# Adjacency graph layers on one Trainium2 core: three edits to the order of work between the second pass and the block layer

## The chip, the cores and the metric

The kernel runs on one core of a Trainium2 chip. The metric is device time in microseconds. The core has five engines that work side by side: TensorE (PE in the profile, its weight loads PEld), VectorE (DVE), ScalarE (ACT), GpSimd (POOL) and SyncE (SP), which here only issues DMAs. [...]

## The reference

Four graph layers over one 2708 x 2708 adjacency matrix `adj` and 2708 x 128 features `x`, each followed by a residual and a layer norm. The edits lie where the first layer ends and the second is prepared, so only these two are shown:

```python
# layer 0: neighbours by distance of z, then a Laplacian product
z = leaky_relu(lap_mul(A, x) @ W1 + b1, 0.1)
S = exp(-dist(z) / 2), kept for the 4 largest of each row
x = layernorm(x + lap_mul(S + A, x) @ W2 + b2)

# layer 1: attention of rank one, normalised by A
XW = X @ W
s_col, s_row = XW @ a[:128], XW @ a[128:]
den = exp(leaky_relu(s_row[:, None] + s_col[None, :], 0.01))
num = A @ den
att = where(num != 0, den / num, 0)
x = layernorm(X + A @ (att @ XW))
```

Layers 2 and 3 are a normalised product with `adj` and a linear map each.

## The kernel before, in words

**Tiles and chunks.** The 2708 nodes are 22 tiles `t` of 128 (the last has 20 nodes) and six chunks `c` of columns: four of 512, one of 384 and one of 276. Chunk index 3 (`C - 3`) holds tiles 12 to 15, index 4 (`C - 2`, the fifth chunk) tiles 16 to 18, and index 5, the last, tiles 19 to 21.

**First and second pass.** The first pass over `adj` finds z and the four neighbours. The second pass (`by_panels`, L189 to L229, with products at L204) multiplies `adj` with the scaled features, chunk by chunk. The work that ends a chunk is not done at once: `end_pass2` (L993) puts it into a list `due` with a number for each step, and one step of the list is taken after each product of the pass. Steps with one number run in the order in which they were put in. Inside this stretch the order on TensorE, VectorE and ScalarE is the order in which the program issues (`manual_schedule`, L1036).

**Ending a chunk.** For each chunk but the last: `finish` copies the accumulator, `norm0` (L797) adds the residual and normalises, `turn` (L814) transposes the rows with TensorE and copies them to `xT` with ScalarE (L821), `find_c` (L869) multiplies them with the column vector into the row of c (`c_row`, L872 and its copy L873) and takes each node's own c out of it (L877). Then for each tile `compare` (L899) writes a 0/1 mask over all columns so far (one compare, L904, and one for ties within the tile, L914), `times_w` (L882) makes the tile's rows of X W (L885 and their copy L886), `rank_rows` (L919) adds up the mask along its rows on ScalarE (L922, a copy with an accumulated sum), and `rank_columns` (L924) does so along columns on TensorE (L927). These sums are the ranks by which nodes are sorted. The masks have four buffers; the PSUM tiles of `mis_tile` have three.

**The last chunk** isn't normalised first. `last_stats` finds mean and variance, GpSimd the power for `rstd_l` (L253), and `last_rc` (L843) corrects two columns of products to c and then r (L847 and L850, twice each). `turn_c` (L861) turns c into a row, which ScalarE copies (L867); `negate_r` follows. Then come `compare`, `rank_rows` and `rank_columns` of tiles 19 and 20, `compare_few` for the last 20 nodes, and the ranks.

**Third pass.** `adj` is read a third time, in 32 half rows of 128 x 1354 through 11 buffers and ten more half rows that stay in SBUF (`res`). `line(n)` multiplies the next n loaded half rows with `lc` (L1387, four column groups) and, where a buffer is used again, issues its next load on SyncE's queue. `own_line(n)` does so with resident ones, without a load. Between them, in an order written out in the list `turns` (L1482), TensorE does what prepares the block layer: `last_xw` makes the last three tiles' rows of X W (transpose L1180, copy L1182, product L1184, copy L1186, a DMA on GpSimd's queue to DRAM), `in_rank_order` and `in_list_order` sort by products with 0/1 matrices (L1228), `counts`, `ranks_known`, `next_weights`.

**Block layer.** `block_layer` (L1639) runs 44 steps of products (L1654), reciprocals on ScalarE, a Newton step on VectorE and products (L1536). Then come three more panel passes for the rest of layers 1 to 3.

## Time and profile before

| | us |
|---|---|
| median of 3 runs | 1071.4 |
| lowest, highest | 1069.7, 1076.45 |
| the profiled execution | 1068.27 |
| its span, first to last instruction | 1066.5 |
| TensorE matmul busy | 983.9 (92%) |
| TensorE weight loads busy | 481.8 (45%) |
| VectorE busy | 637.6 (60%) |
| ScalarE busy | 331.9 (31%) |
| GpSimd busy | 264.9 (25%) |
| mean granted TensorE clock | 0.971 |

The stages that matter here, in us from the start of the span: the second pass's last chunks from about 380 to 437, the last chunk's c, masks and ranks from 437 to 454, the third pass from 454.3 to 506.8, the block layer from 507.5 to 728.8.

In the rows of a timeline, the first number is the start in us, the second the length; then engine, line, operation, the tile written and the tiles read, the shape, and how many instructions are merged. What stands in brackets is the engine's idle time before the row and what ended it. The granted clock is the share of full speed that TensorE is given; it is listed for any stretch one asks for.

### The profile page before, as it was taken

To read this page: it belongs to the slowest core of one execution; us is meant where nothing else is said; L and a number is where in the kernel's file an instruction comes from. 1 tells how busy PE (TensorE), PEld (TensorE's weight loads), DVE (VectorE), ACT (ScalarE), POOL (GpSimd) and SP (SyncE) were. 2 spreads that over 40 slices of the span, in tenths; PEclk is the share of its full clock that TensorE was granted. 3 is DMA by queue.
4 is the path that set the end of the run, shared out by engine and by line. 5 is a ranking of instruction groups with operands and counts; after the bars stand their busy time and mean duration, and the time that the engine had idled before them with its cause. 6 is when DMAs were issued, how large, how long until landed. Compare 5 with 4: busy or idle time off the path is not lost.

```text
span 1066.5 us, 11660 instructions
## 1 busy us (share of the span) xinstructions
PE 983.9 (92%) x3773; PEld 481.8 (45%) x3773; DVE 637.6 (60%) x1363; ACT 331.9 (31%) x609; POOL 264.9 (25%) x339
## 2 busy tenths in 40 slices
PE   0888999999994998799899999999999999999996
PEld 0346544444442556654333333334445544564444
DVE  5985438999943578674798999995121121222222
ACT  0000126555500244612776776663010100010000
POOL 4000000000564565005766443430121100000000
PEclk9989999999997999699999999999999999999998
DMA  9998350000183666587565455456755856484652
GB/s 338 363 340 268 114 160 1 0 1 1 42 278 113 202 184 209 199 357 260 144 172 150 137 141 165 133 169 202 232 189 173 292 181 216 145 276 145 229 166 74
DMA packets 102001, 191.00 MB, mean 179 GB/s; under 512 B 14022, under 2 KB 43342, under 8 KB 101930
## 3 DMA queue, kind: packets, MB, share of 16 engines
q1 hardware_dynamic: 83896, 152.34, 43.1%
q0 software_dynamic: 17728, 37.62, 12.8%
q8 instruction: 32, 0.52, 0.2%
q14 instruction: 39, 0.32, 0.1%
q10 hardware_dynamic: 306, 0.20, 0.1%
HBM read 214.80 MB, written 4.16 MB: 205 GB/s over the span
## 4 chain that ended last, share of the span: by engine, by line
PE 48%; DVE 1%; ACT 1%; issue 0%; DMA 0%; POOL 0%; SPq 0%; POOLq 0%
PE acc L204 27%; PE hacc L1536 10%; PE num L1654 9%; PE mis L285 1%; PE mis L1783 0%; DMA ring<-carry 0%; ACT gb L234 0%; PE mis L1749 0%; DVE inv L1525 0%; PE mis L1779 0%; DVE inv L1528 0%; ACT inv L1511 0%; POOL rstd L253 0%; DVE err L1521 0%; PE mis L1737 0%
## 5 line engine op out<-in xcount | busy, mean ns | idle before, releaser
L1095 POOL DMA_INDIRECT ring<-in_adjT,slot_i x88 | 96.6, 1098 | 93.8 <-PE num L1654 72.1
L1654 PE MATMUL num<-ring,lw 128*64 128x512 f32 (+1 forms) x528 | 111.9, 550 | 4.0 <-DVE err L1521 1.9
L1536 PE MATMUL hacc<-inv,xws 128*128 128x512 f32 (+1 forms) x264 | 111.7, 559 | 1.7 <-ACT xws L1699 1.4
L705 PE MATMUL acc<-zT,z 128*128 128x512 f32 (+2 forms) x252 | 102.2, 552 | 0.0
L1511 ACT ACTIVATE inv<-num,plain 128x1024 f32<-128x1024 f32 x88 | 80.5, 915 | 59.3 <-PE num L1654 38.9
L253 POOL TENSOR_TENSOR rstd<-rstd,minus_half 128x4 f32<-128x4 f32 (+1 forms) x18 | 17.3, 959 | 313.5 <-DVE rstd L252 313.5
L234 ACT COPY gb<-acc 128x512 f32<-128x512 f32 (+2 forms) x18 | 9.6, 534 | 251.1 <-PE acc L204 251.1
L706 ACT COPY key<-acc 128x512 f32<-128x512 f32 (+2 forms) x126 | 67.1, 534 | 55.1 <-PE acc L705 27.7
L204 PE MATMUL acc<-ring,y 128*128 128x512 f32 (+2 forms) x192 | 83.3, 564 | 0.5 <-issue 0.5
L750 POOL DMA_INDIRECT got<-y_rows,where x66 | 70.8, 1073 | 45.8 <-DVE near_sum L763 25.9
L1536 PEld LDWEIGHTS hacc<-inv,xws 128*128 128x128 f32 x264 | 46.5, 189 | 78.7 <-issue 53.4
L1521 DVE TENSOR_TENSOR err<-inv,num 128x1024 f32<-128x1024 f32 x88 | 73.8, 852 | 10.2 <-DMA carry<-m_rows 4.9
L204 PE MATMUL acc<-ring,xs 128*128 128x512 f32 (+2 forms) x192 | 77.6, 547 | 0.0
L1528 DVE SCALAR_TENSOR_TENSOR inv<-gb,g_inv,inv 128x1024 f32<-128x1024 f32 x88 | 77.0, 912 | 0.1
L204 PE MATMUL acc<-ring,carry 128*128 128x512 f32 (+2 forms) x192 | 74.5, 542 | 0.0
L204 PE MATMUL acc<-ring,m_rows 128*128 128x512 f32 (+2 forms) x192 | 74.3, 542 | 0.0
L1525 DVE SCALAR_TENSOR_TENSOR inv<-err,inv 128x1024 f32<-128x1024 f32 x88 | 72.2, 858 | 0.1
L705 PEld LDWEIGHTS acc<-zT,z 128*128 128x128 f32 x252 | 45.8, 190 | 50.4 <-issue 45.0
L1514 ACT ACTIVATE inv<-inv 128x1024 f32<-128x1024 f32 x88 | 67.6, 768 | 2.8
L575 POOL TENSOR_TENSOR slot_e<-near,sim 128x44 f32<-128x44 f32 (+2 forms) x3 | 0.7, 238 | 259.3 <-DVE near L572 259.2
L709 DVE MAX8 near<-key 128x8 f32<-128x2708 f32 x21 | 62.3, 2965 | 2.6 <-ACT key L706 2.6
L1654 PEld LDWEIGHTS num<-ring,lw 128*64 128x64 f32 x528 | 35.6, 136 | 62.4 <-issue 44.6
(378 smaller groups left out, 1368.9 us busy)
## 6 DMA issues: line engine op xcount, KB each, us to landing
ring<-in_adjT SPq DMA_DIRECT2D x74, 1024.0 KB
ring<-in_adjT SPq DMA_DIRECT2D x20, 677.0 KB
ring<-in_adjT SPq DMA_DIRECT2D x17, 768.0 KB
part<-in_adjT SPq DMA_DIRECT2D x12, 1024.0 KB
ring<-in_adjT SPq DMA_DIRECT2D x17, 552.0 KB
more<-in_adjT SPq DMA_DIRECT2D x10, 677.0 KB
res<-in_adjT SPq DMA_DIRECT2D x4, 1280.0 KB
part<-in_adjT SPq DMA_DIRECT2D x3, 768.0 KB
```

The costliest lines, as they stand in the source:

```text
L204: nc.tensor.matmul(accs[c][: lhsT.shape[-1], :w], lhsT=lhsT, rhs=src, start=start, stop=stop)
L705: nc.tensor.matmul(pks[c][:p, : cw[c]], lhsT=z2[:, :p], rhs=zT[:, cs], start=False, stop=True)
L706: nc.scalar.copy(key[:p, cs], pks[c][:p, : cw[c]])
L750: nc.gpsimd.indirect_dma_start(out=got[:p, :], out_offset=None, in_=y2_rows[:, :], in_offset=bass.IndirectOffsetOnAxis(ap=where[:p, t, k : ...
L1095: nc.gpsimd.indirect_dma_start(out=rows[i][:KC, n, :], out_offset=None, in_=adj_half[:, :], in_offset=bass.IndirectOffsetOnAxis(ap=slot_i[ ...
L1511: nc.scalar.activation(inv, num[:, :w], AF.Ln, scale=plain[:, 0:1], bias=plain[:, 1:2])
L1514: nc.scalar.activation(inv, inv, AF.Exp, scale=-1.0)
L1521: nc.vector.tensor_mul(err, inv, num[:, :w])
L1525: nc.vector.scalar_tensor_tensor(inv, err, 2.0, inv, op0=ALU.subtract, op1=ALU.mult)
L1528: nc.vector.scalar_tensor_tensor(inv, gb[:, col : col + w], g_inv[:, q : q + 1], inv, op0=ALU.max, op1=ALU.mult)
L1536: nc.tensor.matmul(haccs[:, o:e], lhsT=xws[:, q, :], rhs=inv[:, o:e], start=(q == 0), stop=(q == NQ - 1))
L1654: nc.tensor.matmul(num[n * (BJ + 2) : (n + 1) * (BJ + 2), o:e], lhsT=lw[:, 2 * q + n, :], rhs=rows[i][:, n, c0 + o : c0 + e], start=True, ...
```

## The change

Three edits to the order, all in the stretch that ends with the third pass.

**Tile 15's sum.** For chunk index `C - 3` the sum along rows of its last tile is no longer put in at its own number but kept in `behind_turn`, and put in for chunk `C - 2` at the number of `find_c`, behind it. (The kernel did so already with the sum of chunk `C - 2`'s last tile, through `behind_last`.)

**Tile 19's compare.** `last_rc` is cut into `last_of`, called once for c and once for r. After c and the start of `turn_c`, `compare_known` compares tile 19 with all columns ahead of the last chunk, whose c is known; `compare` does only the other 128 columns for this tile. r and its negative come behind that.

**X W of the last tiles.** `last_xw` is cut into `turn_last` (transpose and copy) and `last_xw` (product, copy and DMA) of one tile each. Between a tile's transpose and its product stands a half row: the seventh of the loaded ones for tile 19, an own one for each of tiles 20 and 21. The own ones come out of the group of four that followed later.

```diff
-    def last_rc():
-        both = rc_of(C - 1, lambda t: P)
-        for v, dst in ((1, cc), (0, rr)):
-            nc.vector.scalar_tensor_tensor(
-                dst[:, l0:l1], mv[:, l0:l1, 0], w_sum[:, v : v + 1], both[:, v, :], op0=ALU.mult, op1=ALU.subtract
-            )
...
+    unscaled = []
+
+    def last_of(v, dst):
+
+        if not unscaled:
+            unscaled.append(rc_of(C - 1, lambda t: P))
+        nc.vector.scalar_tensor_tensor(
+            dst[:, l0:l1], mv[:, l0:l1, 0], w_sum[:, v : v + 1], unscaled[0][:, v, :], op0=ALU.mult, op1=ALU.subtract
+        )
...
+    def compare_known(t):
+        masks[t] = sum_pool.tile([P, N], BF16, tag="mask", name="mask", bufs=4)
+        nc.vector.tensor_scalar(
+            masks[t][:, : l0 * P], c_row[:, : l0 * P], cc[:, t : t + 1], None, op0=ALU.is_ge
+        )
+
     def compare(t):
         p, o = pw[t], t * P
         s = cc[:p, t : t + 1]
-        mask = masks[t] = sum_pool.tile([P, N], BF16, tag="mask", name="mask", bufs=4)
+        e = l0 * P if t in masks else 0
+        if not e:
+            masks[t] = sum_pool.tile([P, N], BF16, tag="mask", name="mask", bufs=4)
+        mask = masks[t]
         m = split.get(t, o + p)
-        nc.vector.tensor_scalar(mask[:p, :m], c_row[:p, :m], s, None, op0=ALU.is_ge)
+        nc.vector.tensor_scalar(mask[:p, e:m], c_row[:p, e:m], s, None, op0=ALU.is_ge)
...
             at(n + 11, find_c, c)
+            if c == C - 2:
+                for t in behind_turn:
+                    at(n + 11, rank_rows, t)
...
                     behind_last.append(t)
+                elif c == C - 3 and k == len(ts) - 1:
+                    behind_turn.append(t)
                 else:
                     at(n + 16 + 2 * k, rank_rows, t)
...
-            at(n + 3, last_rc)
+            at(n + 3, last_of, 1, cc)
             at(n + 3, turn_c, c)
-            at(n + 3, negate_r)
+            at(n + 3, compare_known, ts[0])
+            at(n + 5, last_of, 0, rr)
+            at(n + 5, negate_r)
...
-        def last_xw():
-            for t in last_ts:
-                p = pw[t]
...
+        last_rows = {}
+
+        def turn_last(t):
...
+            nc.tensor.transpose(pt[:, :p], xs[:p, t, :], ident[:p, :p])
+            xT = last_rows[t] = small.tile([P, P], F32, tag="z", name="xT")
+            nc.scalar.copy(xT[:, :p], pt[:, :p])
+
+        def last_xw(t):
...
+            nc.tensor.matmul(po[:p, :D], lhsT=last_rows[t][:, :p], rhs=wa_sb, start=True, stop=True)
...
         turns = [
-            (line, 4), (blocks_of_edges,), (line, 7), (last_xw,), (in_rank_order, 0), (line, 3),
+            (line, 4), (blocks_of_edges,), (line, 6), (turn_last, T - 3), (line, 1), (last_xw, T - 3),
+            (turn_last, T - 2), (own_line, 1), (last_xw, T - 2), (turn_last, T - 1), (own_line, 1), (last_xw, T - 1),
+            (in_rank_order, 0), (line, 3),
...
-            (add_last_rows, 0), (own_line, 4), (ranks_known,), (line, 2), (own_line, 1), (in_list_order, 0),
+            (add_last_rows, 0), (own_line, 2), (ranks_known,), (line, 2), (own_line, 1), (in_list_order, 0),
```

More of the change, by code (lines that the diff above doesn't have):

```diff
@@ L841, in last_stats @@
         inv_sqrt_of(rstd_l, mv[:, l0:l1, 1], LN_EPS, True)
-    def last_rc():
-        both = rc_of(C - 1, lambda t: P)
-        for v, dst in ((1, cc), (0, rr)):
-            nc.vector.scalar_tensor_tensor(
-                dst[:, l0:l1], mv[:, l0:l1, 0], w_sum[:, v : v + 1], both[:, v, :], op0=ALU.mult, op1=ALU.subtract
-            )
-            nc.vector.scalar_tensor_tensor(
-                dst[:, l0:l1], dst[:, l0:l1], -1.0, rstd_l, op0=ALU.mult, op1=ALU.mult
-            )
+    unscaled = []
[5 more added lines that the diff above has]
+        )
+        nc.vector.scalar_tensor_tensor(
+            dst[:, l0:l1], dst[:, l0:l1], -1.0, rstd_l, op0=ALU.mult, op1=ALU.mult
+        )
     def last_norm():
@@ L897 @@
     split = {T - 2: (T - 1) * P // 2}
+    def compare_known(t):
+        masks[t] = sum_pool.tile([P, N], BF16, tag="mask", name="mask", bufs=4)
+        nc.vector.tensor_scalar(
+            masks[t][:, : l0 * P], c_row[:, : l0 * P], cc[:, t : t + 1], None, op0=ALU.is_ge
+        )
     def compare(t):
@@ L991 @@
     behind_last = []
+    behind_turn = []
     def end_pass2(c, acc):
@@ L1173 @@
         last_norm()
-        def last_xw():
-            for t in last_ts:
-                p = pw[t]
-                pt = mis_tile()
-                nc.tensor.transpose(pt[:, :p], xs[:p, t, :], ident[:p, :p])
-                xT = small.tile([P, P], F32, tag="z", name="xT")
-                nc.scalar.copy(xT[:, :p], pt[:, :p])
-                po = mis_tile()
-                nc.tensor.matmul(po[:p, :D], lhsT=xT[:, :p], rhs=wa_sb, start=True, stop=True)
-                row = small.tile([P, P], F32, tag="junk", name="row")
-                nc.scalar.copy(row[:p], po[:p, :D])
-                nc.gpsimd.dma_start(xw_rows[t * P : t * P + p, :], row[:p])
+        last_rows = {}
+        def turn_last(t):
+            p = pw[t]
+            pt = mis_tile()
+            nc.tensor.transpose(pt[:, :p], xs[:p, t, :], ident[:p, :p])
+            xT = last_rows[t] = small.tile([P, P], F32, tag="z", name="xT")
+            nc.scalar.copy(xT[:, :p], pt[:, :p])
+        def last_xw(t):
+            p = pw[t]
+            po = mis_tile()
+            nc.tensor.matmul(po[:p, :D], lhsT=last_rows[t][:, :p], rhs=wa_sb, start=True, stop=True)
+            row = small.tile([P, P], F32, tag="junk", name="row")
+            nc.scalar.copy(row[:p], po[:p, :D])
+            nc.gpsimd.dma_start(xw_rows[t * P : t * P + p, :], row[:p])
         def whole(dst, src, n):
```

## The prediction

> **What bounds the kernel now.** First the chain of waits. It is nearly all TensorE work and can be followed back only to 517 us, through the block layer (L1654, L1536), a steady sequence of products.

> ```profile
> PE 48%; DVE 1%; ACT 1%; issue 0%; DMA 0%; POOL 0%; SPq 0%; POOLq 0%
> ```

> Nothing after 517 us is edited, so what counts is when the block layer's first product starts, at 507.50. Before that I read the timeline backwards. From 461.5 to 506.8 TensorE goes through its queue with almost no wait that another engine ended (the waits list has 1.0 us for L1184 in all), so that stretch is bound by TensorE's own order, and what it gains shifts the start. Ahead of it lie two places where TensorE stands. The first is in the fifth chunk, around 422 us:

> ```profile
> 420.89 1.80 ACT L922 ACTIVATE junk<-mask 128x1920 bf16<-128x1920 bf16 x1
> ...
> 422.69 0.25 ACT L886 COPY xwe<-mis 128x129 f32<-128x129 f32 x1
> 422.84 1.92 ACT L922 ACTIVATE junk<-mask 128x2048 bf16<-128x2048 bf16 x1
> ...
> 424.74 0.47 ACT L821 COPY xT<-mis 128x384 f32<-128x384 f32 x1
> ...
> 425.27 1.65 PE L872 MATMUL mis<-xT,w_c 128*128 128x384 f32 x2 [2.65 <-ACT xT L821]
> ```

> The transposes for xT ended at 420.65, but their copy stands behind a mask sum, and TensorE waits 2.65 us. The second is the X W stretch of the third pass:

> ```profile
> 461.54 0.33 PE L1180 MATMUL mis<-ident,xs 128*128 128x128 f32 x1
> 462.22 0.49 PE L1184 MATMUL mis<-w_att,xT 128*128 128x128 f32 x2 [0.35 <-ACT xT L1182]
> ...
> 463.24 0.49 PE L1184 MATMUL mis<-w_att,xT 128*128 128x128 f32 x2 [0.41 <-ACT xT L1182]
> ...
> 464.48 2.04 PE L1228 MATMUL js<-val_q,hot_in 128*128 128x44 f32 x12
> ...
> 466.45 3.03 PE L1387 MATMUL acc<-ring,lc 128*32 128x339 f32 x24
> ...
> 470.87 1.91 PE L1387 MATMUL acc<-ring,lc 128*32 128x339 f32 x24
> ```

> The last two rows are the same work, three half rows: 3.03 us and 1.91. The table of stretches says why (columns: stretch, length, busy time of PE, PEld, DVE, ACT, POOL, granted clock, DMA share, GB/s):

> ```profile
> 420.97:424.38 3.41, 1.25 (x18) 0.67 (x17) 3.20 (x11) 3.41 (x5) 0.83 (x1) 1.00 0.85 292
> 424.38:427.79 3.41, 2.52 (x5) 1.66 (x6) 0.35 (x4) 1.31 (x4) 0.00 (x0) 0.50 0.65 230
> 427.79:431.21 3.42, 3.42 (x10) 2.61 (x9) 3.42 (x9) 1.07 (x2) 0.00 (x0) 0.50 0.25 51
> ...
> 461.93:465.34 3.41, 2.43 (x16) 1.77 (x16) 3.34 (x8) 1.27 (x6) 1.36 (x3) 1.00 1.02 421
> 465.34:468.75 3.41, 3.41 (x27) 1.84 (x29) 3.34 (x8) 0.00 (x0) 0.36 (x1) 0.50 1.03 418
> ```

> After a stretch of 3.41 us with gaps the next one runs at half clock: two after the 2.65 us wait, one after the X W stretch. A gap thus costs twice.

> [...]

> **The change, part by part.** Counted by engine, TensorE, ScalarE, GpSimd and SyncE issue the same instructions as before; VectorE has one more. No DMA is added or moved past another; only waits on load slots of two or three half rows change.

> *A. Sum of tile 15 (L922, 128x2048) behind the copies of xT and of the fifth chunk's row of c.* xT starts when L886 ends, at 422.69+0.25=422.94 instead of 424.74: 1.80 us earlier, and L872 at 423.47. From 425.27 to the copy of the last chunk's accumulator (436.22) TensorE had 10.95 us, 5.94 of them at half clock: 5.01+2.97=7.98 us of work at full clock. From 423.47, with the windows where they are: both half-clock windows stay: 0.91+6.83/2=4.33 done by 431.21, 3.65 left, end 434.86, gain 1.36. Only one stays (TensorE is then busy all through 424.38 to 427.79): 0.91+1.71 done by 427.79, end 433.15, gain 3.07. None: end 431.45. What was behind the sum waits for it now: the three copies of xwe (L886) and the sums of tiles 16 to 18, 2.0 to 2.4 us each. ScalarE had 6.0 us of idle time between 424.74 and 439.01 (1.74, 2.71, 1.38, 0.18), which takes the sum's 1.9 us; but it becomes the bound if TensorE gets fast: laying its rows end to end from the copy of c (424.9) brings the last chunk's xT to 435.35 with no half-clock window and 436.2 with one, against 439.01. So A gains 1.3, 2.8 or 3.7 us. I take 2.8: the 0.65 us still to wait leaves a gap in the first window, so I expect one to be lost. The xwe copies come later by up to a sum, but their PSUM buffers (three) are next wanted by L800 and L818, some 5 us on: no wait.

> *B. Tile 19 in two pieces, r behind it.* Before, VectorE computed c and r, then idled 0.82 us until c's row was copied, then compared 2560 columns. Rows of the timeline:

> ```profile
> 441.07 0.16 DVE L850 SCALAR_TENSOR_TENSOR cc<-cc,rstd_l 128x3 f32<-128x3 f32 x1 [0.44 <-POOL rstd_l L253]
> ...
> 442.17 0.39 ACT L867 COPY hT<-mis 128x276 f32<-128x276 f32 x1 [1.38 <-PE mis L866]
> 442.59 1.55 DVE L904 TENSOR_SCALAR mask<-hT,cc 128x2560 bf16<-128x2560 f32 x1 [0.82 <-ACT hT L867]
> ```

> Now 2432 columns (1.48 us, as tile 18 took) start at 441.3 and end at 442.78, just past the row's copy (442.56); 128 more take 0.28 (the shortest L904), own ties 0.35, and the three small operations of r 0.65 with their gaps, so tile 20 starts near 444.0 instead of 444.33. The extra instruction costs 0.21 (0.28 less the 0.07 that 128 more columns cost in the long one); cover for it and for r is the 0.82 us wait. Without that cover B would lose 0.2. Tile 19's sum on ScalarE starts 1.1 us earlier, but the ranks need VectorE's compares of tile 20 and the last 20 rows, so only VectorE's 0.35 us reaches the first half row. Taken 0.35, between -0.2 and 0.6.

> *C. Own half rows between the X W products.* L1180, L1182, L1184 and L1186 keep their number; one ring half row and two own ones move between them. At full clock a half row takes 0.57 us (four took 2.28 from 481.24), and a switch from half rows to another product about 0.38 (483.27 to 483.65). Before: from the first transpose to the first rank product 464.48-461.54=2.94, plus the three half rows elsewhere, 1.71: 4.65. After: transpose, half row, then L1184 after its drain 1.23 us later; then own row and drain, 1.35 and 1.30; then 0.25 to the rank product: 4.13. Gain 0.52. The copies of xT (0.27) and GpSimd's three row DMAs lie under the half rows; the gathers that read those rows start 22 us later (487.65). Were every half row and switch serial with the old chain, it would be 2.94+3x(0.57+0.38+0.1)=6.09, a loss of 1.44. Then the clock: with TensorE busy about nine tenths through that stretch I expect 465.34 to 468.75 at full clock, which saves half of 3.41, 1.7 (0 if not).

> Is there room downstream? Half-row loads saturate the DMA (1.02 of its share); each takes about 1.7 us. Their landings move with the front by A and B; TensorE catches up by C's 2.2 at most. The tightest used half row had landed some 3.6 us before its use by my reading of the semaphores, so loads don't become the wait. Waits of GpSimd and SyncE there are on TensorE and move with it.

> Sum: 2.8+0.35+0.5+1.7=5.35. The profiled execution took 1068.27 us (span 1066.5 and 1.8 around it), so 1062.9 for it; it lies 3.1 below the median of 1071.4, so the forecast is 1066.0.

> **Rivals.** *Order alone:* the gaps shrink but the windows still fall on them, so no half-clock stretch goes. For it: 2.43 us busy of 3.41 lost the clock at 461.93, and A leaves about as little in its window. Against: C fills its gaps. Gain 1.3+0.35+0.5=2.15: 1069.2.
> *More half-clock windows:* [...]a changed rhythm can lose stretches that are kept now. Each costs 1.7 us; from two more than now on the 2.15 is gone: 1071.4-2.15+3.4=1072.7, slower. For it: half clock already holds for four windows from 441.45. Against: every edit takes idle time off TensorE.
> *The gain is swallowed:* between 494.99 and 496.73 TensorE stands without a named cause, and VectorE's first slot list and a load issue start right after. If a transfer sets that moment and doesn't move, about 1.7 us are lost again: 5.35-1.7=3.65, 1067.7. The DMA is far from full there, which speaks against.

> **The numbers.** Forecast as summed 0.45, order alone 0.25, swallowed 0.15, more windows 0.10, larger than summed (A at 3.7 and the half clock of 441 to 455 shortened by another window) 0.05. The bounds go from a gain of 0.5 to one of 7.5; the runs shown lie from 1.7 below their median to 5 above it. The range is 1062.5 to 1072. One per cent, 10.7 us, is about what a measurement of this kernel can tell from no change. All cases lie within it; I leave 0.05 for faster and 0.03 for slower, for what the trace doesn't show.

> **What would show it.** In the changed profile: xT's copy directly behind the first xwe copy and TensorE's wait ahead of L872 down from 2.65 to about 0.9; one half-clock window instead of two there; VectorE's wait for c's row gone; the first three ring half rows behind the X W products in 1.9 us, not 3.0; the block layer's first product near 502 instead of 507.50, and everything after it as long as before. It is wrong if that product hasn't moved by at least 1 us, if a wait on a load or on the xwe copies appears on TensorE, or if more than 20 us of half clock lie between 420 and 470 (23.9 before).

## The result and the profile after

| | before | after |
|---|---|---|
| median of 9 runs each, same chip | 1073.2 us (1069.7 to 1078.21) | 1065.15 us (1062.09 to 1070.15) |
| ratio, 95% interval | | 0.9925, 0.9903 to 0.9947 |
| the profiled execution, its span | 1068.27, 1066.5 us | 1065.13, 1063.3 us |
| TensorE at half clock in the span, and from 410 to 475 us | 63.9, 23.9 us | 63.3, 13.65 us |

The change made the kernel 0.75% faster, within the one per cent that was called no change. The forecast was 1066.0, a ratio of 0.9950 to the median of 1071.4: a little less gain than the interval holds. That 1066.0 lies within 1 us of the measured median is partly luck, since the median of the kernel before moved from 1071.4 (three runs) to 1073.2 (nine). The two profiled executions differ by only 3.14 us, less than the ratio says. One reason shows at once: tile 15's rank columns, ahead of every edit, start at 421.52 us before and at 423.89 after, so the execution after came 2.37 us late into the stretch. Lengths are therefore counted from there: to the block layer's first product it is 507.50 - 421.52 = 85.98 us before and 502.29 - 423.89 = 78.40 after, 7.58 less. (Lines move: L872 is L874 now, L904 is L915 and the new L903, L1184 is L1208, L1387 is L1411, L1654 is L1680, L1536 is L1562.) The two ends of the first part of that length, before:

```profile
421.52 0.53 PE L927 MATMUL rk<-ones_b,mask 128*128 128x1 bf16 x15 [0.40 <-DVE mask L904]
...
436.22 0.39 ACT L1000 COPY hT<-acc 128x276 f32<-128x276 f32 x1 [1.38 <-PE acc L770]
```

The chain that ended last is still mostly TensorE work, 51% of the span:

```profile
PE 51%; DVE 2%; issue 2%; DMA 1%; ACT 1%; SPq 1%; another core or an unknown queue 0%; POOL 0%; POOLq 0%
```

The timeline of the fifth chunk, after:

```profile
423.89 0.53 PE L938 MATMUL rk<-ones_b,mask 128*128 128x1 bf16 x15 [0.40 <-DVE mask L915]
...
425.07 0.25 ACT L888 COPY xwe<-mis 128x129 f32<-128x129 f32 x1
425.21 0.49 ACT L821 COPY xT<-mis 128x384 f32<-128x384 f32 x1
425.75 0.91 PE L874 MATMUL mis<-xT,w_c 128*128 128x384 f32 x2 [0.76 <-ACT xT L821]
426.70 0.48 ACT L875 COPY hT<-mis 128x384 f32<-128x384 f32 x1 [1.00 <-PE mis L874]
427.08 1.91 ACT L933 ACTIVATE junk<-mask 128x2048 bf16<-128x2048 bf16 x1
...
433.79 0.39 ACT L1012 COPY hT<-acc 128x276 f32<-128x276 f32 x1
```

xT's copy stands directly behind the xwe copy, the sum of 2048 columns behind both, TensorE's wait is 0.76 us instead of 2.65, and the product takes 0.91 instead of 1.65. The table of stretches on the clock's own grid (stretch, length, busy time of PE, PEld, DVE, ACT, POOL, granted clock, DMA share, GB/s) shows why:

```profile
421.91:425.33 3.42, 2.68 (x26) 1.48 (x24) 3.31 (x10) 3.42 (x7) 0.00 (x0) 1.00 0.85 318
425.33:428.74 3.41, 2.99 (x13) 2.38 (x14) 2.87 (x12) 2.41 (x3) 0.83 (x1) 1.00 0.84 261
428.74:432.15 3.41, 3.41 (x44) 2.80 (x43) 3.41 (x7) 3.36 (x7) 0.00 (x0) 1.00 0.90 310
```

Both half-clock windows are gone. From the rank columns to the copy of the last chunk's accumulator it takes 433.79 - 423.89 = 9.90 us instead of 14.70. VectorE on tile 19, after:

```profile
438.65 0.16 DVE L852 SCALAR_TENSOR_TENSOR cc<-cc,rstd_l 128x3 f32<-128x3 f32 x1 [0.45 <-POOL rstd_l L253]
438.85 1.49 DVE L903 TENSOR_SCALAR mask<-hT,cc 128x2432 bf16<-128x2432 f32 x1
440.25 0.28 DVE L915 TENSOR_SCALAR mask<-hT,cc 128x128 bf16<-128x128 f32 x1
```

The wait of 0.82 us for c's row is gone. And TensorE in the X W stretch, after:

```profile
458.20 0.33 PE L1200 MATMUL mis<-ident,xs 128*128 128x128 f32 x1
458.46 0.78 PE L1411 MATMUL acc<-y_place,lc 128*32 128x339 f32 x8
459.16 0.49 PE L1208 MATMUL mis<-w_att,xT 128*128 128x128 f32 x2
...
461.57 0.38 PE L1208 MATMUL mis<-w_att,xT 128*20 128x128 f32 x2
461.89 1.53 PE L1252 MATMUL js<-val_q,hot_in 128*128 128x44 f32 x12
463.35 1.91 PE L1411 MATMUL acc<-ring,lc 128*32 128x339 f32 x24
```

No row there waits any more, and the three ring half rows take 1.91 us where they took 3.03. What was not expected is the start of the block layer. Before:

```profile
507.50 4.31 PE L1654 MATMUL num<-ring,lw 128*64 128x512 f32 x20 [0.66 <-issue]
...
515.26 2.66 PE L1654 MATMUL num<-ring,lw 128*64 128x512 f32 x8 [0.81 <-DMA ring<-carry]
517.85 2.54 PE L1536 MATMUL hacc<-inv,xws 128*128 128x512 f32 x6
```

After:

```profile
502.29 4.31 PE L1680 MATMUL num<-ring,lw 128*64 128x512 f32 x20 [0.66 <-DVE lw L1397]
508.47 0.78 PE L1680 MATMUL num<-ring,lw 128*64 128x330 f32 x4 [1.88 <-DVE err L1547]
510.96 3.73 PE L1680 MATMUL num<-ring,lw 128*64 128x512 f32 x8 [1.71 <-DMA ring<-carry]
514.61 2.54 PE L1562 MATMUL hacc<-inv,xws 128*128 128x512 f32 x6
...
519.56 2.54 PE L1562 MATMUL hacc<-inv,xws 128*128 128x512 f32 x6
```

and the stretches of the same place:

```profile
507.25:510.66 3.41, 0.78 (x4) 0.20 (x4) 3.41 (x5) 3.38 (x5) 2.90 (x3) 1.00 0.39 65
510.66:514.08 3.42, 3.12 (x7) 1.50 (x8) 3.42 (x5) 0.53 (x2) 2.62 (x3) 0.50 0.69 204
```

Two waits fall into one window and the next one runs at half clock: the eight wide products take 3.73 us (2.66 before), and the first sum (`hacc`) comes 12.33 us behind the first product instead of 10.35.

### The profile page after: what moved, and what is told of

Its sections match the earlier page's. It is cut to its first block, busy times and chain, and to the rows that moved or that the text cites. A ratio compares the mean times of both kernels' runs of the same rounds, so it can differ in the third digit from the quotient of the medians.

```text
span 1063.3 us, 11660 instructions
## 1 busy us (share of the span) xinstructions
PE 984.6 (93%) x3773; PEld 481.4 (45%) x3773; DVE 637.5 (60%) x1364; ACT 331.9 (31%) x609; POOL 268.5 (25%) x339
## 4 chain that ended last, share of the span: by engine, by line
PE 51%; DVE 2%; issue 2%; DMA 1%; ACT 1%; SPq 1%; another core or an unknown queue 0%; POOL 0%; POOLq 0%
PE acc L204 28%; PE hacc L1562 10%; PE num L1680 9%; DMA ring<-in_adjT 1%; PE acc L1411 1%; PE mis L285 1%; PE mis L1809 0%; SPq L1440 0%; ACT gb L234 0%; PE mis L1136 0%; PE js L1252 0%; PE mis L1775 0%; DVE err L1547 0%; DVE inv L1551 0%
## 5 line engine op out<-in xcount | busy, mean ns | idle before, releaser
L1680 PE MATMUL num<-ring,lw 128*64 128x512 f32 (+1 forms) x528 | 112.0, 556 | 4.2 <-DVE err L1547 1.9
L1562 PE MATMUL hacc<-inv,xws 128*128 128x512 f32 (+1 forms) x264 | 111.7, 559 | 1.6 <-ACT inv L1540 1.3
L253 POOL TENSOR_TENSOR rstd<-rstd,minus_half 128x4 f32<-128x4 f32 (+1 forms) x18 | 17.3, 960 | 315.1 <-DVE rstd L252 315.1
L1562 PEld LDWEIGHTS hacc<-inv,xws 128*128 128x128 f32 x264 | 46.5, 189 | 78.9 <-issue 53.6
L204 PE MATMUL acc<-ring,y 128*128 128x512 f32 (+2 forms) x192 | 81.2, 552 | 0.5 <-issue 0.5
L1547 DVE TENSOR_TENSOR err<-inv,num 128x1024 f32<-128x1024 f32 x88 | 73.4, 852 | 10.2 <-DMA res<-in_adjT 4.0
L204 PE MATMUL acc<-ring,xs 128*128 128x512 f32 (+2 forms) x192 | 78.5, 552 | 0.0
L204 PE MATMUL acc<-ring,carry 128*128 128x512 f32 (+2 forms) x192 | 74.5, 542 | 0.0
L204 PE MATMUL acc<-ring,m_rows 128*128 128x512 f32 (+2 forms) x192 | 74.3, 542 | 0.0
L1680 PEld LDWEIGHTS num<-ring,lw 128*64 128x64 f32 x528 | 36.3, 137 | 61.7 <-issue 42.4
```

The costliest lines, as they stand in the source:

```text
L204: nc.tensor.matmul(accs[c][: lhsT.shape[-1], :w], lhsT=lhsT, rhs=src, start=start, stop=stop)
L1547: nc.vector.tensor_mul(err, inv, num[:, :w])
L1562: nc.tensor.matmul(haccs[:, o:e], lhsT=xws[:, q, :], rhs=inv[:, o:e], start=(q == 0), stop=(q == NQ - 1))
L1680: nc.tensor.matmul(num[n * (BJ + 2) : (n + 1) * (BJ + 2), o:e], lhsT=lw[:, 2 * q + n, :], rhs=rows[i][:, n, c0 + o : c0 + e], start=True, ...
```

## The experiments

The theory was that each gap costs twice, once as a wait and once as a half-clock window behind it; the rivals were that only the order counts, that another engine takes over as the bound, or that the gain is given back behind it. All twelve kernels, those before and after included, were profiled, these two twice; the other ten were each timed beside the kernel before as well. The lengths in us, read from each trace's timeline (copy: of the last chunk's accumulator; few: rank columns of the last 20 rows; the sums: first and second group of `hacc` behind the block layer's first product), with half-clock windows of 3.41 us in brackets:

| kernel | rank columns 15 to copy | copy to few | first half row to block layer | to 1st sum | to 2nd sum | block layer to end | ratio to before |
|---|---|---|---|---|---|---|---|
| before | 14.70 (2) | 11.41 | 53.21 (1) | 10.35 | 16.95 | 559.04 | |
| before, second profile | 14.61 (2) | 11.52 | 56.32 (3) | 10.38 | 17.07 | 559.07 | |
| A alone | 9.90 (0) | 11.18 | 53.45 (1) | 10.35 | 16.97 | 555.99 | 0.9962 (0.9945 to 0.998) |
| A's wait filled | 13.33 (0) | 11.81 | 53.42 (1) | 10.36 | 16.83 | 558.40 | 0.9969 (0.995 to 0.9987) |
| B alone | 13.44 (1) | 10.81 | 56.06 (3) | 10.36 | 17.40 | 559.16 | 0.9993 (0.9972 to 1.0013) |
| C alone | 14.69 (2) | 11.43 | 50.59 (0) | 11.90 | 17.09 | 557.81 | 0.9971 (0.9944 to 0.9999) |
| C's waits filled | 14.22 (2) | 11.54 | 51.40 (0) | 10.62 | 17.53 | 559.66 | 0.9977 (0.9958 to 0.9997) |
| after | 9.90 (0) | 10.76 | 51.08 (0) | 12.33 | 17.27 | 561.03 | 0.9925 (0.9903 to 0.9947) |
| after, second profile | 11.58 (1) | 10.80 | 50.31 (0) | 11.76 | 16.87 | 560.42 | |
| after, block start filled | 9.89 (0) | 10.80 | 50.49 (0) | 10.34 | 17.03 | 560.06 | 0.9946 (0.9922 to 0.9969) |

The windows in the fourth column are those behind the X W products alone (this column starts at the third pass's first half row); the four at about 437 to 455 us, in every row of the table but one (five with A's wait filled), are not in it. The quotient of the medians can differ from the ratio on record by 0.1 to 0.3% (1070.79/1071.65 = 0.9992 for C's waits filled), so the lengths carry the argument and the ratios only bound it.

**The parts alone.** Each kernel has one of the three edits of the diff shown above and nothing else of it.

A: `behind_turn` alone.

```diff
             at(n + 11, find_c, c)
+            if c == C - 2:
+                for t in behind_turn:
+                    at(n + 11, rank_rows, t)
...
```

> Part A alone: only tile 15's mask sum goes behind the copies of xT and of the fifth chunk's row of c. Measure: from tile 15's rank columns to the block layer's first product (85.98 us before, 78.40 with the whole change). Theory (gap and clock): TensorE's 2.65 us wait ahead of L872 falls to about 0.8, both half-clock windows after it (6.83 us) go, the last chunk's accumulator is copied 4.8 us earlier in relation to the rank columns and the stretch falls to about 81.2; the median falls by about 4.8 us, ratio 0.9955. Rival (order alone): one or both half-clock windows stay, the stretch falls by 1.4 to 3.1 us. Rival (ScalarE becomes the bound, as the prediction capped it): 3.7.

Measured: the stretch to the block layer is 81.19 us, both windows are gone, and the accumulator's copy comes 4.80 us earlier; the ratio is 0.9962, about 4.1 us. So in this execution A alone gives what the theory said, and not the 3.7 at which the prediction capped it. The timed ratio (a gain of 2.1 to 5.9 us) can't tell the two apart; the trace does. ScalarE takes over no part of it here: the last chunk's xT comes 2.79 us behind the accumulator's copy in this kernel as in the one before.

B: `last_of`, `compare_known` and the two-piece `compare` alone.

```diff
-            at(n + 3, last_rc)
+            at(n + 3, last_of, 1, cc)
             at(n + 3, turn_c, c)
-            at(n + 3, negate_r)
+            at(n + 3, compare_known, ts[0])
+            at(n + 5, last_of, 0, rr)
+            at(n + 5, negate_r)
```

> Part B alone: tile 19 compared in two pieces, r behind the first. Theory: VectorE's wait for the row of c (0.82 us) is filled, the tile's rank work starts 0.3 to 0.7 us earlier and the stretch from tile 15's rank columns to the block layer's first product falls from 85.98 by that much; both half-clock windows at about 424 to 431 stay, since nothing ahead of them is changed. In the timed runs it can't be told from no change (0.05%). Rival: the split costs its extra instruction, 0.2 us more.

Measured: copy to few is 10.81 us where it was 11.41 and 11.52, a gain of 0.6 to 0.7. The total can't be told from no change. One expectation failed: only one half-clock window lay at 423 us, although nothing ahead of it was changed. And three lay behind the X W products instead of one, so the stretch grew to 86.98.

C: `turn_last`, `last_xw` and the order of `turns` alone.

```diff
-            (line, 4), (blocks_of_edges,), (line, 7), (last_xw,), (in_rank_order, 0), (line, 3),
+            (line, 4), (blocks_of_edges,), (line, 6), (turn_last, T - 3), (line, 1), (last_xw, T - 3),
+            (turn_last, T - 2), (own_line, 1), (last_xw, T - 2), (turn_last, T - 1), (own_line, 1), (last_xw, T - 1),
+            (in_rank_order, 0), (line, 3),
...
```

> Part C alone: half rows between the last X W products. Theory: the three ring half rows behind those products take 1.9 us instead of 3.03, the half-clock window that fell on them is gone, and the stretch from tile 15's rank columns to the block layer's first product falls from 85.98 by about 2.1 us (0.5 by order, 1.7 by clock); median 2 us less, ratio 0.998. Rival (order alone): 0.5 us, a half-clock window still lies there or elsewhere in the stretch. Rival (half rows and switches serial with the old chain): 1.4 us more.

Measured: 83.38 us, no window behind the X W products; 2.62 us less from the first half row to the block layer than in the first profile of before. The ratio, 0.9971, is about 3.1 us. The first sum comes 1.55 us later behind the first product, with a half-clock window, as after.

**The kernel before, once more.**

> The kernel before, profiled a second time. It tells whether the half-clock windows at 424 to 431, 441 to 455 and 465 to 469 us belong to the kernel or to where the window happened to lie. Theory (gaps long enough lose the clock wherever the window lies): windows within 3.4 us of the same places, stretch within 1 us of 85.98. Rival (chance of the window's phase): one of them missing or a new one, and the stretch 1.7 us or more away from 85.98.

Measured: the windows recur at the same places, but behind the X W products there are three, not one, and the stretch is 89.11 us, 3.1 longer. So the rival held, chance of the window's phase. Its table of stretches:

```profile
459.25:462.67 3.42, 2.38 (x16) 1.66 (x15) 3.35 (x7) 1.30 (x6) 1.25 (x3) 1.00 1.02 423
462.67:466.08 3.41, 3.41 (x23) 2.01 (x26) 3.34 (x9) 0.00 (x0) 0.47 (x1) 0.50 1.03 409
466.08:469.49 3.41, 3.41 (x22) 2.16 (x14) 3.31 (x9) 0.00 (x0) 0.00 (x0) 0.50 1.01 405
469.49:472.91 3.42, 3.42 (x24) 1.63 (x28) 1.24 (x2) 0.00 (x0) 0.00 (x0) 0.50 1.02 418
```

Nearly the same gaps (2.38 us busy of 3.42, where it was 2.43 of 3.41) now cost three windows, 3 x 1.7 = 5.1 us. Of the five profiles without C and with the X W waits open, three had one window and two had three. The profile that the prediction was made from was one of the cheap ones.

**Clock or order.** Two kernels leave the order as before and fill the waits with unread products of the unit matrix:

```diff
+    def fill(n):
+        if not filled:
+            filled.append(js_pool.tile([P, CW], F32, tag="places", name="fill"))
+        for _ in range(n):
+            nc.tensor.matmul(filled[0][:, :P], lhsT=ident, rhs=ident, start=True, stop=True)
...
+            if c == C - 2:
+                at(n + 11, fill, 20)
             at(n + 11, find_c, c)
```

> The kernel before, with the mask sum left where it was, and 20 products of the unit matrix with itself (128x128, result never read) put on TensorE ahead of L872, so that the 2.65 us wait is filled with work and not shortened. It tells how much of part A is the clock and how much is the order. Theory (gap costs twice): L872 still starts 3.75 us after tile 15's rank columns, but both half-clock windows after it are gone, and from L872 to the copy of the last chunk's accumulator it takes 8.0 us instead of 10.95; stretch to the block layer's first product about 83.0 if one window lies at the X W products, about 86 if three do. Rival (the windows have another cause, for example the DMA load): both stay, 10.9 us.

Measured, in its timeline (L880 is the product L872 of before):

```profile
414.25 4.63 PE L818 MATMUL fill<-ident 128*128 128x128 f32 x40
416.54 0.47 ACT L829 COPY xT<-mis 128x384 f32<-128x384 f32 x1
418.71 0.81 PE L880 MATMUL mis<-xT,w_c 128*128 128x384 f32 x2
...
426.65 0.39 ACT L1008 COPY hT<-acc 128x276 f32<-128x276 f32 x1
```

The 20 products (two records each) took 4.63 us, twice what was meant, so L880 started 5.40 us behind the rank columns and not 3.75, and the stretch to the block layer fell only to 85.2 us, not to the 83.0 expected. But both windows are gone, and from L880 to the accumulator's copy it takes 426.65 - 418.71 = 7.94 us; the theory said 8.0, the rival 10.9. So in A the clock is worth 10.95 - 7.94 = 3.0 us, and the order the other 1.8. This kernel was profiled once, but each of the five profiles with this wait open has at least one window there. The kernel is faster than before (0.9969) though it only adds work, 1.65 us of which stands in the way.

For part C, one such product ahead of each X W product:

```diff
                 po = mis_tile()
+                fill(1)
                 nc.tensor.matmul(po[:p, :D], lhsT=xT[:, :p], rhs=wa_sb, start=True, stop=True)
```

> The kernel before, with one unread product of the unit matrix (0.25 us) ahead of each of the three X W products, and no half row moved. It tells how much of part C is the clock. Theory: the waits for xT (0.35, 0.25 and 0.41 us) are filled, no half-clock window falls behind the X W products, where the kernel before showed one or three; from the first X W transpose to the block layer's first product it takes 44.2 to 44.8 us, against 45.96 or 49.17 before and 43.91 with part C. Rival (only the moved half rows keep the clock): one or three windows as before, 46 or 49 us.

Measured: 44.45 us, no window. Its stretches:

```profile
459.74:463.15 3.41, 3.08 (x20) 2.22 (x20) 3.38 (x6) 1.30 (x6) 1.15 (x2) 1.00 1.01 416
463.15:466.57 3.42, 3.42 (x39) 2.19 (x39) 3.32 (x9) 0.00 (x0) 0.57 (x1) 1.00 1.03 408
```

3.08 us busy of 3.41 kept the clock where 2.38 and 2.43 lost it, and all five profiles with these waits open have at least one window there. So of part C the clock is 45.96 - 44.45 = 1.5 us where one window lay, and 49.17 - 44.45 = 4.7 where three did. The rest is order: from the first X W transpose to the first rank product part C takes 461.89 - 458.20 = 3.69 us with three half rows in it, where before it took 2.94 and the half rows 1.71 elsewhere: 0.96.

**What is given back at the block layer's start.**

> The changed kernel, profiled a second time. Theory: the stretch from tile 15's rank columns to the block layer's first product repeats within 1 us of 78.40, with no half-clock window behind L874 and none behind the X W products; the block layer's first 12.33 us are partly chance: 10.35 to 12.4[...]. Rival (the give-back belongs to the change): 12.3 again, with the half-clock window and a DMA wait of 1.7 us.

Measured: 79.36 us, one window behind L874, and 11.76 us to the first sum with a window again (507.84). The one behind L874 is a matter of where the grid lies:

```profile
419.09:422.50 3.41, 2.25 (x24) 1.27 (x23) 3.27 (x10) 3.24 (x7) 0.25 (x1) 1.00 0.83 311
422.50:425.91 3.41, 3.41 (x7) 2.32 (x8) 2.25 (x10) 1.93 (x2) 0.58 (x1) 0.50 0.85 212
```

Here the 0.76 us wait and a 0.40 us wait at tile 15's rank columns share a window, which has 2.25 us of work; after, the window from 421.91 had 2.68 and kept the clock. At the block layer the DMA wait was 0.82 us this time, as before, so its 1.71 was chance; the window recurred. Of the 1.98 us given back in the first profile, 3.73 - 2.66 = 1.07 is the clock and 0.90 that transfer; of the 1.41 in the second, the clock is 4.05 - 2.66 = 1.39. To see what it costs, 7 and 3 unread products were put ahead of the two waits, and nothing else was added to the change:

```diff
+            def keep_warm(n):
+                for _ in range(n):
+                    nc.tensor.matmul(haccs[0][:, :P], lhsT=ident, rhs=ident, start=True, stop=True)
...
+                    if i == 1:
+                        haccs[0] = ops.tile([P, 3 * CW], F32, tag="hacc", name="hacc")
+                        keep_warm(7)
                     find_num(i, "narrow")
+                    if i == 1:
+                        keep_warm(3)
...
```

> The whole change, and 7 and 3 unread products of the unit matrix with itself ahead of the two waits at the block layer's start (1.88 us for err, then for the carry rows), nothing else. All four profiles with part C so far had a half-clock window there (block layer's first product to its first sum 11.8 to 12.3 us), all five without C had none (10.35). Theory (the change moves the gap onto a whole window, and the clock is the give-back): with the gap filled no window is lost there and it takes 10.2 to 10.7 us to the first product of inv and xws; median about 1.5 us under the changed kernel's, ratio to the kernel before about 0.991. Rival (the give-back is a transfer that comes late): 11.3 us or more though no window is lost.

Measured in its timeline:

```profile
502.14 4.31 PE L1680 MATMUL num<-ring,lw 128*64 128x512 f32 x20 [0.66 <-ACT m_rows L1432]
506.38 1.83 PE L1701 MATMUL hacc<-ident 128*128 128x128 f32 x14
508.32 0.78 PE L1680 MATMUL num<-ring,lw 128*64 128x330 f32 x4
509.03 0.94 PE L1701 MATMUL hacc<-ident 128*128 128x128 f32 x6
509.91 2.64 PE L1680 MATMUL num<-ring,lw 128*64 128x512 f32 x8
512.48 2.54 PE L1562 MATMUL hacc<-inv,xws 128*128 128x512 f32 x6
...
517.34 1.90 PE L1680 MATMUL num<-ring,lw 128*64 128x512 f32 x6 [0.77 <-issue]
519.17 2.54 PE L1562 MATMUL hacc<-inv,xws 128*128 128x512 f32 x6
```

The window is gone and the first sum comes at 10.34 us, so the clock was the cause of the part that recurs. But the kernel was not shown to be faster than the change alone (0.9946 against 0.9925), and the row at 517.34 says why: TensorE now waits 0.77 us there, which the changed kernel did not. The second sum comes 17.03 us behind the first product, against 17.27 and 16.87 in the two profiles of after and 16.95 before. What looks like a give-back of 1.4 to 2 us was absorbed one step later: before, TensorE waits there as well, 0.67 us at 522.62.

**Keeping the clock from 437 to 455 us as well.** In all profiles up to here four windows (five once) follow the waits around the last chunk's masks. Four kernels put unread products into those waits on top of the change.

```diff
+            at(n + 2, fill, 3)
             at(n + 2, turn, c, True)
...
+            at(n + 3, fill, 4)
             at(n + 3, last_of, 1, cc)
+            at(n + 3, fill, 7)
             at(n + 3, turn_c, c)
...
+                at(n + 5 + k, fill, 5 if k == 0 else 8)
                 at(n + 5 + k, rank_columns, t)
...
+            at(n + 3 + len(ts), fill, 2)
             at(n + 3 + len(ts), compare_few)
```

> The whole change, and 45 unread products of the unit matrix with itself spread over TensorE's waits from the last chunk's transposes to the last rank columns (3, 4, 7, 5, 8, 8, 8 and 2 of them), where in all runs so far four windows (13.65 us) of half clock follow. Theory: these windows go too; from the last 20 rows' rank columns to the first half row it takes 3.5 to 5 us instead of 6.66, and the stretch from tile 15's rank columns to the block layer's first product falls from 78.4 to 75 to 77; median 2 to 4 us under the changed kernel's. Rival (VectorE and ScalarE bound that stretch, half clock costs nothing there): 6.66 stays, and the unread products cost 0 to 1 us.

The next has this and, at the block layer's start, `keep_warm(14)` and `keep_warm(6)` in place of 7 and 3:

> As f2_fill_ranks, and 14 and 6 unread products ahead of the two waits at the block layer's start (1.88 us for err, 0.8 to 1.7 us for the carry rows). Theory (the give-back there is a half-clock window that the gap opens[...]): from the block layer's first product to the first hacc product 10.35 to 10.6 us and no half-clock window, instead of 12.33. Rival (the give-back is the DMA wait): 11.3 us or more without a half-clock window.

The next has 1, 2, 3, 2, 4 and 1 products in those places (the fourth and fifth ahead of the rank columns of tiles 19 and 20), 7 and 3 at the block layer:

> The whole change, and unread products in both places in the size of the waits (0.25 us each): 1, 2, 3, 2, 4, 4, 4 and 1 from the last chunk's transposes to the last rank columns, 7 and 3 at the block layer's start. Theory (the half clock costs where TensorE is the bound, and VectorE takes over soon behind it): no half-clock window between 410 and 520 us, last accumulator's copy to the last 20 rows' rank columns 10.5 to 10.8 us (11.1 when oversized), from there to the first half row 5.1 instead of 6.66, the block layer's first sum 10.2 to 10.7 us behind its first product; stretch from tile 15's rank columns to the block layer's first product 76.5 to 77.5; median 2 to 4 us under the changed kernel's, ratio to the kernel before 0.988 to 0.990. Rival (loads and VectorE give it all back): stretch 78.4 or more, ratio as for the changed kernel, 0.9925.

The last has 1, 2, 3, 4, 4 and 1, none at the block layer, and `fill(4)` between tile 20's two groups of rank columns:

> The whole change, unread products (0.25 us each) in TensorE's waits from the last chunk's transposes to the last rank columns only (1, 2, 3, 4, 4, 1), and 4 more between the two halves of tile 20's rank columns, where f4_fill_sized still stood for 1.13 us and lost two windows behind it. Theory: no half-clock window from 430 to 500 us, from the last 20 rows' rank columns to the first half row 5.1 us instead of 6.66, then VectorE and the loads give part of it back: from those rank columns to the first X W transpose 12.3 to 12.8 us against 13.65 and 13.07 in the two profiles of the changed kernel; median 0.5 to 1.5 us under the changed kernel's, ratio to the kernel before 0.990 to 0.992. Rival (all given back): 13 us or more, ratio 0.9925 or more.

(The first and third of these expectations count two places too many: tiles 19 and 20 have one each, so it was 29 and 13 products.) Measured:

| | windows, 437 to 455 | copy to few | few to first half row | rank columns 15 to block layer | median | ratio to before |
|---|---|---|---|---|---|---|
| after | 4 | 10.76 | 6.66 | 78.40 | 1065.15 | 0.9925 (0.9903 to 0.9947) |
| oversized | 1 | 11.11 | 6.31 | 79.27 | 1062.48 | 0.9923 (0.9895 to 0.995) |
| oversized, both places | 0 | 11.12 | 5.08 | 77.25 | 1060.09 | 0.9898 (0.9867 to 0.993) |
| sized, both places | 2 | 10.76 | 6.66 | 78.06 | 1063.1 | 0.9886 (0.9842 to 0.993) |
| sized, tile 20 too | 1 | 10.76 | 6.14 | 79.05 | 1061.24 | 0.9926 (0.9902 to 0.9951) |

(The stretches of 79.27 and 79.05 have a window behind L874 in them, as the second profile of after has. The medians of before, timed beside each, are 1073.2, 1070.84, 1070.84, 1071.65 and 1069.47, so only the ratios compare. The ratio of 0.9886 rests on six runs, and the quotient of its medians is 0.9920.)

None of these four expectations came true as a whole. The oversized fill left one window and gave 6.31 and 79.27 us, where 3.5 to 5 and 75 to 77 were expected; the next kernel has the same fill there and left none, so that difference is chance. But 14 products take 3.39 us in a wait of 1.88, and its block layer came to the first sum at 11.67 us though no window was lost; it can't tell the clock from a late transfer, and the kernel with 7 and 3 can. The sized fill left two windows and the 6.66. The last left one, gave 6.14 instead of 5.1 and 12.88 to the first X W transpose, above the 12.3 to 12.8 expected, and its ratio is the rival's.

The timeline of the oversized fill in both places, which kept the clock throughout, shows what comes next:

```profile
442.48 1.09 PE L1149 MATMUL mis<-ident,gb_col 128*128 128x128 f32 x8
444.78 0.36 PE L1178 MATMUL mis<-c_part_head,ones_f 128*128 128x11 f32 x2 [1.21 <-DVE c_part_head L1172]
445.00 1.74 PE L1149 MATMUL mis<-ident,gb_col 128*128 128x128 f32 x14
446.87 2.48 PE L1424 MATMUL acc<-ring,lc 128*32 128x339 f32 x32
450.38 0.39 PE L1178 MATMUL mis<-c_part_first,ones_f 128*128 128x44 f32 x2 [1.03 <-DVE c_part_first L1172]
```

The 22 transposes take 2.83 us where they took 5.20, but VectorE ends two waits of 1.21 and 1.03 us. From the accumulator's copy to the first X W transpose it is 11.12 + 5.08 + 7.39 = 23.59 us against 10.76 + 6.66 + 6.99 = 24.41 and 23.87 in the two profiles of after. Four windows would cost 4 x 1.7 = 6.8 us where TensorE is the bound, and 0.3 to 0.8 came back, so half clock there hides mostly behind other waits, of which VectorE ends these two. All four intervals overlap that of the change: no version was shown to beat it.

## Why the prediction was right, and where its sizes were off

**The bound and the mechanism** were right. Of what the prediction named to look for, all but two signs are there: the copies in their new order, the wait at 0.76 us, no wait for c's row, 1.91 us for the ring half rows. At about 424 us no window was left, where one was expected, and what lies behind the block layer's first product did not stay as long as before. That this product starts at 502.29, as forecast, is partly luck: this execution came 2.37 us late into the stretch, and the gain ahead of it was 7.58. The two kernels that fill the waits without shortening them show that half of the reasoning, "a gap costs twice", and not just its outcome.

**Term A was mis-sized: 2.8 taken, 4.8 measured.** Two of the three cases worked out are confirmed: with one window left it gave 14.70 - 11.58 = 3.1 (3.07 worked out), with none 4.80 (4.77); both windows together (1.36) never stayed. Two choices went wrong. One window was expected to stay; of the eight profiles with A, five have none there and three have one. And the case with none was capped at 3.7 by ScalarE. That cap put the last chunk's xT at 435.35; it came at 436.58, less the 2.37 us by which this execution was late, 434.21. The three sums from 427.08 on and the copy of the accumulator start 2.22, 2.16 and 2.33 us apart, with a copy between each, since a sum and the read of its accumulator overlap (427.08 + 1.91 = 428.99, and the read starts at 428.89). ScalarE is nearly full there but still waits 0.18 us for the transposes ahead of that xT.

**Term B**: 0.35 taken, 0.6 to 0.7 measured alone and 0.4 on top of A (copy to few, 11.18 to 10.76 and 10.80), inside the bound of 0.6 or just past it. The split and r are covered by the wait, as argued.

**Term C**: order 0.52 taken, 0.96 measured. The 0.38 us for a switch was counted from 483.27, where the second half of a half row's products starts, so most of it lay within the 0.57 already counted: from the start of a half row to the product behind it, it took 0.70, 0.71 and 0.59 us, not 0.95. The clock: 1.7 taken, 1.5 measured where one window lay. But one profile was taken for the kernel. In two of five there are three windows, which C removes as well, so its mean worth is higher: the five without it average 54.49 us from the first half row to the block layer, and the four with C and nothing filled ahead of it (C alone, the two of after, the block start filled) 50.62, a gain of 3.87. That is 1.65 above the 2.2 taken, the largest excess of the three terms. How often a run has one window there and how often three, five profiles can't tell.

**The rivals.** Order alone is refuted, serial half rows too, and the wait at 494.99 without a named cause swallowed nothing: the first product moved by 7.58. More half-clock windows was the right thing to fear, but in another place: the prediction said that everything behind the block layer's first product would be as long as before. It isn't: the end comes 561.03 and 560.42 us behind it, not 559.04 and 559.07. The window at 510 us has no part in that, since by the second sum it has cost nothing (17.27 and 16.87 us, against 16.95 and 17.07). What remains lies at 960 to 975 us, where no line was edited: both profiles of after have two half-clock windows there, those of before have one. That is no effect of the order of work itself: the kernel before with C's waits filled has two as well, and two of the seven profiles with the whole change have one. The last section shows what the number goes with.

Put together: 3.87 for A (14.33, the mean of the five with its wait open, less 10.46, the mean of the three with the whole change), 0.65 for B (with what A adds to that stretch), 3.87 for C, less 1 to 2 behind it (560.06, 560.42 and 561.03 against 559.05), is 6.4 to 7.4; the ratio says 8.0, between 5.7 and 10.4. The prediction's bounds ended at 7.5. Luck kept its error small: what it took too low for A and C was in part lost again behind the block layer, where it expected nothing. Timed alone, the parts add up to the whole within their intervals of some 0.2 to 0.3% each: 0.38% + 0.07% + 0.29% = 0.74%, where 0.75% was measured; that it agrees so closely is chance.

## What to carry to other kernels

Read the granted clock on its own grid before pricing a wait, and take a second profile: the same X W gaps cost one window or three, the wait left behind part A none or one. In this kernel a wait of 2.65 us, and three of 1.03 us together, cost 3.0 and 1.5 to 4.7 us of half clock besides their own length. Filling the wait with idle products got the clock back, shortening it got both (3.0 and 4.8 us at part A's wait); but check what ends the next wait, since four half-clock windows in front of other engines' waits were worth only 0.3 to 0.8 us here. Clock was lost and won where nothing was edited, too: at 960 to 975 us both profiles of after have two half-clock windows and those of before one, and at 423 us B alone has one where before has two.

## What the runs showed of the hardware

**The place on the grid goes with the number of windows.** For five places, the fourteen traces give how far a fixed point of the kernel lies behind an edge of the grid:

| place, with its waits open, and the point measured | us behind the edge, and half-clock windows that follow |
|---|---|
| fifth chunk, wait of 2.65 us; tile 15's rank columns | 0.55, 0.56, 0.74, 1.53: two; 3.10: one |
| the same with A, wait of 0.76 us | 1.30, 1.31, 1.43: one; 1.66 to 2.94 (five profiles): none |
| X W products in the order before; first transpose | 2.76, 2.77, 3.03: one; 3.13, 3.38: three |
| block layer's start; its first product | 0.01 to 1.33 (six): none; 1.85 to 2.29 (five): one |
| 960 to 975 us; the L204 product 4.86 us ahead of the first of the last tile's (961.55 before) | 0.62 to 1.69 (seven): one; 1.87 to 2.64 (six): two; 3.01: none |

In the last row the end comes 103.3 us behind that point with no window, 104.7 to 105.1 with one and 106.4 to 106.8 with two. So the loss at one place goes by where the grid lies: B alone, at 3.10 in the first row, lost one window and not two though nothing ahead of it was edited. It also tests the fills: the filled wait of the fifth chunk lies at 0.98, between 0.74 and 1.53, the filled X W products at 3.35, between 3.13 and 3.38, the filled block layer's start at 1.85 and 2.28, and none of them lost a window. There the fill and not the place kept the clock. For part C itself that isn't shown, since its first transposes lie at 1.71 to 2.75, where no profile with the order before lies. No run shifted a place on purpose.

**A window that is busy throughout can lose the clock too.** The prediction ties half clock to a window with gaps. But before, from 967.10 to 970.51 us TensorE is busy in the records all the time, 3.41 us of 3.41, and the next window still runs at half clock:

```profile
967.10:970.51 3.41, 3.41 (x12) 1.20 (x11) 0.57 (x2) 0.76 (x2) 0.00 (x0) 1.00 0.00 0
970.51:973.93 3.42, 3.42 (x11) 2.39 (x11) 2.81 (x16) 0.00 (x0) 0.00 (x0) 0.50 0.00 0
```

About 2.7 of the 3.4 us are products over the last tile, with 20 rows instead of 128 (L204, 20x512). Windows made mostly of transposes went both ways: behind the one after from 445.81 to 449.22 us, 3.00 us busy of which 2.58 are transposes (L1136), the clock stayed at half; in the oversized fill in both places the one from 442.30 to 445.72 us, 2.21 us busy of which 1.81 are transposes, kept it. Nor is there one busy time that parts the windows: behind A alone's from 455.99 to 459.41, with 2.70 us busy, the clock was lost, while before it stayed through two windows from 509.71 to 516.54 with 2.10 and 2.05. No run here separated the causes.
